# Joining the key and query weights in a routed cross-attention kernel, and moving setup's statistics

## The chip, the core and the metric

The kernel runs on one core of a Trainium2 chip. The time is device microseconds (us) of that core. The engines are PE (TensorE, matrix multiplies; its weight loads are shown as PEld), DVE (VectorE), ACT (ScalarE), POOL (GpSimd) and SP (SyncE, which here only issues transfers). Each engine works through its own list of instructions in order and waits on semaphores for the others. SP, ACT and POOL issue transfers; the queue of SP is q1 in the profile, that of ACT is q10, that of POOL is q0.

## What is computed

There are 8 batches of 512 tokens with 256 features, and 64 context rows per batch. A layer norm of x is followed by attention over the context rows, a router over three experts, the experts, and a gate. All is in 32-bit floats. Cut to what matters here:

```python
nx = layer_norm(x, ln_gamma, ln_beta)
q = nx @ Wq
k = context @ Wk
v = context @ Wv
weights = softmax(einsum('bth,bph->btp', q, k) * H ** (-0.5))
evidence = einsum('btp,bph->bth', weights, v)
combined = concatenate([nx, evidence, cond])
router_probs = softmax(combined @ router_W + router_b)
h = silu(einsum('btc,ecr->bter', combined, e_w1) + e_b1)
expert_out = einsum('bter,erh->bteh', h, e_w2) + e_b2
routed = sum(expert_out * router_probs)
g = sigmoid(silu(combined @ gate_w1 + gate_b1) @ gate_w2 + gate_b2)
out = x + g * (routed @ out_w + out_b)
```

## The kernel before

The batches are taken in pairs (j = 0 to 3). Before the pairs there is a setup, which makes what all pairs use and does the first pair's layer norm, transposes, scores and softmax. Then each pair runs `gate_layer`, `expert_layer` for three experts, and `outputs`; the next pair's layer norm, scores and softmax are placed between these by hand. The order of all engines' instructions is the order in which the program writes them (`manual_schedule`); no planner moves them.

Queries are never made. The scores nx Wq (context Wk)^T are computed as nx times a small matrix per batch, mr, with mr = Wq Wk^T context^T. It has 64 columns for each batch (512 in all), and three further columns of router weights stand beside them. The kernel before makes it in two steps:

- `context_transposes` (L270) turns the context with PE into ctxT, in two halves; DVE copies the first half out of PSUM, ACT the second.
- `project_keys` (L303) multiplies ctxT by Wk, again by halves, into two PSUM banks: eight matmuls of 128x256. ACT copies them to kT (L315).
- `wq_transposes` (L285) transposes Wq with four PE transposes; ACT copies them to wqT (L292).
- `project(wqT, kT, keep_m, "m")` (L1087) makes mr with four matmuls of 128x512; DVE copies each half (L318).

`project` (L294) is also used for v = Wv context (L1078). One 32-bit matmul appears in the trace as two records.

Setup's other work on these lines: `statistics(b, t0, t1)` (L451) runs mean and variance of token blocks t0 to t1 of batch b on DVE, `deviation` (L461) takes the square root on ACT, `normalize` (L464) normalizes x in place on DVE, and `transpose_x` (L486) turns it with PE and scales it on the way out of PSUM, half on DVE (L477) and half on ACT (L481). `small_transposes` (L257) turns the bias rows and cond; `router_anchor` (L324) makes one router row per batch, which POOL writes to memory and reads back spread over the partitions (L332, L333). `scores` (L523) multiplies x by mr. `value_weights` (L622) multiplies v by the second part of the first-layer weights; its router columns go through memory and back on POOL's queue (vrd and vr, L337 and L339) and are read by `router_logits` (L570). `load_table` (L117) runs a one-element activation so that its table is in place early.

PSUM banks in setup are taken in turn by `either` (L244: banks 1, 2, 0, 3) and `misc` (L103: banks 4, 6, 7). The weights and the transposed context live in tiles that later hold the hidden layer and second-layer weights: wk_sb, wq_sb, wqT, wv_sb in one (`scr_w`), kT and the router row in another (`scr_k`). The loads for later weights into the same tiles, `load_anchor(1)` and `load_second(0)`, wait until these are read.

The first transfers are written so: SP issues the context (two halves), x of batch 0, Wq, x of batch 1, then the first-layer weights; ACT issues Wk and Wv; POOL issues the small rows. PE runs seven dummy matmuls first (`wake`, L250).

Of the kernel before, what the change touches and what calls it, by code (L numbers as in the profile page):

```python
# [9 lines left out]
AF = mybir.ActivationFunctionType  # L10
# [6 lines left out]
def kernel(  # L17
# [50 lines left out]
    nc = tc.nc  # L68
    P = 128
    B, T, H = x.shape  # L70
    CT = context.shape[1]
    E, C3, RH = e_w1.shape
    KH = H // P
    NT = T // P
# [22 lines left out]
    def bank(i, name):  # L97
        return psum.tile([P, 512], F32, tag=f"b{i}", name=name)
# [4 lines left out]
    def misc(name):  # L103
        spare.append(spare.pop(0))
        return bank(spare[-1], name)
# [6 lines left out]
    ident = const.tile([P, P], F32, tag="ident", name="ident")  # L112
# [4 lines left out]
    def load_table(func):  # L117
        nc.scalar.activation(warm_t, warm_t, func)
# [5 lines left out]
    def load_x(b):  # L124
        x_sb[b] = xpool.tile([P, NT, H], F32, tag="x", name=f"x_{b}")
        nc.sync.dma_start(x_sb[b], x[b].rearrange("(t p) d -> p t d", p=P))
# [5 lines left out]
    def rows_of(w):  # L132
        return w.rearrange("(k p) n -> p k n", p=P)


    NX = B * CT // P
    HK = KH * RH

    def scratch(i, g, name):
        return h_tile(i, g, name).rearrange("p r t -> p (r t)")  # L140

    def by_k(flat, n):
        return flat.rearrange("p (k n) -> p k n", n=n)

    scr = scratch(1, 2, "scr_ctx")
    ctx_sb, ctxT = by_k(scr[:, :HK], H), by_k(scr[:, HK:], B * CT)
    scr = scratch(1, 1, "scr_w")
    wk_sb, wq_sb, wqT, wv_sb = (by_k(scr[:, i * KH * H : (i + 1) * KH * H], H) for i in range(4))
    scr = scratch(0, 2, "scr_k")
    kT = by_k(scr[:, :HK], B * CT)  # L150
    rrow = scr[:E, HK : HK + B]
    scr = scratch(0, 0, "scr_wa0")
    wa = {0: by_k(scr[:, :HK], RH), E: by_k(scr[:, HK : HK + KH * H], H)}
    scr = scratch(1, 0, "scr_small")
# [80 lines left out]
    vT = const.tile([P, KH, B * CT], F32, tag="vT", name="vT")  # L235
# [8 lines left out]
    def either(name):  # L244
        turn[0] += 1
        return bank((1, 2, 0, 3)[turn[0] % 4], name)
# [10 lines left out]
    def small_transposes():  # L257
        pt = either("pt_rows")
        nc.tensor.transpose(pt[:, :NR], rows, ident[:NR, :NR])
        nc.vector.tensor_copy(cols, pt[:, :NR])  # L260
        pt = either("pt_cond")
        for k in range(KH):
            nc.tensor.transpose(
                pt[:, k * B : (k + 1) * B], cond_sb[:, k * P : (k + 1) * P], ident[:B, :B]
            )
        nc.vector.tensor_copy(
            condT[:, :, :B], pt[:, : KH * B].rearrange("p (k b) -> p k b", b=B)
        )

    def context_transposes():  # L270
        for d in range(2):
            if d:
                wake(1)
            pt = either(f"pt_ctx_{d}").rearrange("p (k c) -> p k c", k=KH)
            for k in range(KH):
                for t in range(NX // 2):
                    nc.tensor.transpose(
                        pt[:, k, t * P : (t + 1) * P],
                        ctx_sb[:, d * (NX // 2) + t, k * P : (k + 1) * P],
                        ident,  # L280
                    )
            half = slice(d * NX // 2 * P, (d + 1) * NX // 2 * P)
            (nc.scalar.copy if d else nc.vector.tensor_copy)(ctxT[:, :, half], pt)

    def wq_transposes():  # L285
        pt = either("pt_wq")
        for k in range(KH):
            for i in range(KH):
                nc.tensor.transpose(
                    pt[:, k * H + i * P : k * H + (i + 1) * P], wq_sb[:, i, k * P : (k + 1) * P], ident  # L290
                )
        nc.scalar.copy(wqT.rearrange("p k n -> p (k n)"), pt)  # L292

    def project(w_sb, src, evacuate, name):  # L294
        for m in range(KH):
            ps = either(f"ps_{name}_{m}")
            for k in range(KH):
                nc.tensor.matmul(  # L298
                    ps, w_sb[:, k, m * P : (m + 1) * P], src[:, k, :], start=(k == 0), stop=(k == KH - 1)
                )  # L300
            evacuate(m, ps)

    def project_keys():  # L303

        ps = [either(f"ps_k_{m}") for m in range(KH)]
        for d in range(2):
            half = slice(d * NX // 2 * P, (d + 1) * NX // 2 * P)
            for m in range(KH):
                for k in range(KH):
                    nc.tensor.matmul(  # L310
                        ps[m][:, half], wk_sb[:, k, m * P : (m + 1) * P], ctxT[:, k, half],
                        start=(k == 0), stop=(k == KH - 1),
                    )
        for m in range(KH):
            nc.scalar.copy(kT[:, m, :], ps[m])  # L315

    def keep_m(m, ps):
        nc.vector.tensor_copy(mr[:, m, :, :CT], ps.rearrange("p (b c) -> p b c", c=CT))  # L318
# [5 lines left out]
    def router_anchor():  # L324
        ps = misc("ps_rb")
        for k in range(KH):
            nc.tensor.matmul(
                ps[:E, :B], rw[:, 2 * KH + k, :], condT[:, k, :B], start=(k == 0), stop=(k == KH - 1)
            )
        nc.vector.tensor_scalar(rrow, ps[:E, :B], rb_c, None, ALU.add)  # L330
        rbd = dram.tile([E, B], F32, tag="rbd", name="rbd")
        nc.gpsimd.dma_start(rbd, rrow)  # L332
        nc.gpsimd.dma_start(rbias, rbd.partition_broadcast(P))  # L333
# [117 lines left out]
    def statistics(b, t0, t1):  # L451
        j, i = b // 2, b % 2
        if b % 2 == 0 and t0 == 0:
            S["mv", j] = work.tile([P, 2, NT, nc.vector.BN_AGGR_DIM], F32, tag="mv", name=f"mv_{j}")
            S["sd", j] = work.tile([P, 2, NT], F32, tag="sd", name=f"sd_{j}")
        for t in range(t0, t1):
            st = work.tile([P, nc.vector.BN_STATS_DIM], F32, tag="st", name=f"st_{b}_{t}")
            nc.vector.bn_stats(st, x_sb[b][:, t, :])
            nc.vector.bn_aggr(S["mv", j][:, i, t, :], st)

    def deviation(j, i):  # L461
        nc.scalar.activation(S["sd", j][:, i, :], S["mv", j][:, i, :, 1], AF.Sqrt, bias=eps_t)

    def normalize(b):  # L464
        mv, sd = (S[n, b // 2][:, b % 2] for n in ("mv", "sd"))
        rstd = work.tile([P, NT], F32, tag="rstd", name=f"rstd_{b}")
        nc.vector.reciprocal(rstd, sd)
        xn = x_sb[b]
        for t in range(NT):
            nc.vector.tensor_scalar(  # L470
                xn[:, t, :], x_sb[b][:, t, :], mv[:, t, 0:1], rstd[:, t : t + 1], ALU.subtract, ALU.mult
            )
        S["xn", b] = xn

    def scale_x(b, k, src, vector):
        if vector:
            nc.vector.tensor_scalar(  # L477
                S["nxT", b][:, k, :], src, gamma_c[:, k : k + 1], beta_c[:, k : k + 1], ALU.mult, ALU.add
            )
        else:  # L480
            nc.scalar.activation(  # L481
                S["nxT", b][:, k, :], src, AF.Identity, bias=beta_c[:, k : k + 1],
                scale=gamma_c[:, k : k + 1],
            )

    def transpose_x(b):  # L486
        xn = S.pop(("xn", b))
        S["nxT", b] = npool.tile([P, KH, T], F32, tag="nxT", name=f"nxT_{b}")
        for k in range(KH):
            pt = misc(f"pt_x_{b}_{k}")  # L490
            for t in range(NT):
                nc.tensor.transpose(pt[:, t * P : (t + 1) * P], xn[:, t, k * P : (k + 1) * P], ident)
            scale_x(b, k, pt, k % 2 == 0)
# [562 lines left out]
    with tc.manual_schedule(engines=None):  # L1056
        ctx_rows = context.flatten_outer_dims().rearrange("(t p) d -> p t d", p=P)
        for d in range(2):
            half = slice(d * NX // 2, (d + 1) * NX // 2)
            nc.sync.dma_start(ctx_sb[:, half, :], ctx_rows[:, half, :])  # L1060
        nc.scalar.dma_start(wk_sb, rows_of(Wk))
        nc.scalar.dma_start(wv_sb, rows_of(Wv))
        load_x(0)
        nc.sync.dma_start(wq_sb, rows_of(Wq))
        load_x(1)
        for g in (E, 0):
            load_first(g)
# [3 lines left out]

        wake(7)
        context_transposes()
        project_keys()
        statistics(0, 0, NT)
        deviation(0, 0)
        normalize(0)
        project(wv_sb, ctxT, lambda m, ps: nc.scalar.copy(vT[:, m, :], ps), "v")  # L1078
        small_transposes()
        wq_transposes()  # L1080
        transpose_x(0)
        router_anchor()
        statistics(1, 0, NT)
        deviation(0, 1)
        normalize(1)
        load_table(AF.Exp)
        project(wqT, kT, keep_m, "m")  # L1087
        combine_weights(E)
        value_weights(0, E)
        spread_router_rows(0)  # L1090
# [131 lines left out]
```

## Time and profile before

| what | value |
|---|---|
| median of 3 runs | 476.01 us (475.64 to 476.08) |
| profiled execution, its own time | 476.25 us |
| span of that execution | 474.5 us |
| ACT busy | 46% of the span |
| POOL busy | 16% of the span |
| transfers | 35.27 MB, mean 74 GB/s over the span |
| transfers in the first 20 us | 6.41 MB, mean 320 GB/s |

The span is the stretch from the first to the last instruction of the profile; the execution's own time is longer by what lies around it. Busy time on PE counts pipelined matmuls whose ends are modelled. In setup (the first 25 us) the groups below have these mean durations for one instruction or record; PE records of successive matmuls overlap, so PE is better read by the distance of their starts.

| line, engine, what | shape | count to 30 us | mean ns |
|---|---|---|---|
| L310 PE matmul, keys | 128x256 | 16 | 394 |
| L298 PE matmul, v | 128x512 | 8 | 592 |
| L298 PE matmul, m | 128x512 | 8 | 605 |
| L289 PE transpose, wq | 128x128 | 4 | 286 |
| L458 DVE statistics | 128x256 | 8 | 400 |
| L459 DVE aggregate | 128x6 | 8 | 182 |
| L470 DVE normalize | 128x256 | 8 | 410 |
| L477 DVE scale | 128x512 | 2 | 806 |
| L318 DVE copy to mr | 128x512 | 2 | 687 |
| L462 ACT square root | 128x4 | 2 | 297 |
| ACT table load | | 4 | 1283 |

### The profile page before, as it was taken

To read this page: it belongs to the slowest core of one execution; us is meant where nothing else is said; L and a number is where in the kernel's file an instruction comes from. 1 tells how busy PE (TensorE), PEld (TensorE's weight loads), DVE (VectorE), ACT (ScalarE), POOL (GpSimd) and SP (SyncE) were. 2 spreads that over 40 slices of the span, in tenths; PEclk is the share of its full clock that TensorE was granted. 3 is DMA by queue.
4 is the path that set the end of the run, shared out by engine and by line. 5 is a ranking of instruction groups with operands and counts; after the bars stand their busy time and mean duration, and the time that the engine had idled before them with its cause. 6 is when DMAs were issued, how large, how long until landed. Compare 5 with 4: busy or idle time off the path is not lost.

```text
span 474.5 us, 4652 instructions
## 1 busy us (share of the span) xinstructions
PE 469.6 (99%) x1451; PEld 225.1 (47%) x1451; DVE 353.4 (74%) x649; ACT 218.4 (46%) x391; POOL 78.2 (16%) x96
## 2 busy tenths in 40 slices
PE   9999999999999999999999999999999999999997
PEld 7654646435454444445454444445454444444454
DVE  2755766989989555889989565898989624697982
ACT  3555656557321546748320456758221365458000
POOL 5227032300062200000062200000042300000020
PEclk9999999999999999999999999999999999999999
DMA  8988330048311840342111750252011560000013
GB/s 285 369 126 159 59 134 1 0 103 104 33 22 22 168 145 0 78 101 44 17 24 22 155 155 2 62 115 46 18 22 22 83 185 0 1 0 1 0 22 67
DMA packets 118120, 35.27 MB, mean 74 GB/s; under 512 B 104732, under 2 KB 115088, under 8 KB 117584
## 3 DMA queue, kind: packets, MB, share of 16 engines
q1 hardware_dynamic: 114736, 27.02, 28.4%
q0 software_dynamic: 1472, 7.18, 4.7%
q10 hardware_dynamic: 1888, 0.79, 0.6%
q8 instruction: 11, 0.18, 0.2%
q14 instruction: 13, 0.11, 0.1%
HBM read 27.57 MB, written 7.40 MB: 74 GB/s over the span
## 4 chain that ended last, share of the span: by engine, by line
PE 94%; DVE 4%; issue 1%; ACT 0%; ACTq 0%
PE ps_u L656 42%; PE ps_z L656 18%; PE ps_y L656 15%; PE ps_vw L631 5%; PE ps_gu L656 3%; PE ps_s L531 3%; PE ps_w2o L416 2%; PE ps_gz L656 1%; DVE h L930 1%; PE ps_wake L255 1%; PE ps_k L310 1%; DVE h L739 1%; PE ps_gy L656 1%; PE ps_v L298 1%; PE ps_ar L354 0%
## 5 line engine op out<-in xcount | busy, mean ns | idle before, releaser
L739 DVE TENSOR_TENSOR h<-h,pb 128x512 f32<-128x512 f32 x96 | 61.9, 693 | 10.5 <-ACT h L689 10.5
L656 PE MATMUL ps_u<-h,w2o 128*128 128x512 f32 x144 | 63.9, 593 | 0.0
L656 PE MATMUL ps_u<-nxT,w 128*128 128x512 f32 x112 | 55.6, 607 | 0.0
L689 ACT ACTIVATE h<-h,abias 128x512 f32<-128x512 f32 x72 | 49.2, 718 | 8.7 <-DVE h L695 8.2
L656 PE MATMUL ps_z<-wT,vw 64*128 64x512 f32 x104 | 49.5, 605 | 0.0
L962 POOL TENSOR_TENSOR yb<-yb,xb 128x512 f32<-128x512 f32 x14 | 19.1, 1365 | 149.5 <-DVE yb L961 145.2
L656 PE MATMUL ps_z<-h,w2s 128*128 128x512 f32 x96 | 42.8, 595 | 0.2 <-DVE r L945 0.2
L698 ACT COPY h<-ps_u 128x512 f32<-128x512 f32 x48 | 28.0, 583 | 32.2 <-PE ps_u L656 31.9
L656 PEld LDWEIGHTS ps_u<-h,w2o 128*128 128x128 f32 x144 | 27.1, 190 | 31.3 <-issue 29.7
L695 DVE TENSOR_TENSOR h<-h,ps_y 128x512 f32<-128x512 f32 x24 | 16.4, 683 | 28.5 <-PE ps_y L656 28.5
L930 DVE TENSOR_TENSOR h<-h,h 128x1024 f32<-128x1024 f32 x24 | 34.3, 1483 | 0.0
L656 PEld LDWEIGHTS ps_u<-nxT,w 128*128 128x128 f32 x112 | 19.9, 189 | 29.7 <-issue 22.8
L689 ACT ACTIVATE h<-ps_u,abias 128x512 f32<-128x512 f32 x24 | 16.5, 687 | 30.4 <-PE ps_z L656 30.4
L656 PE MATMUL ps_y<-nxT,w 128*128 128x512 f32 x56 | 28.6, 592 | 0.0
L656 PE MATMUL ps_z<-T,ws 128*128 128x512 f32 x56 | 28.6, 592 | 0.0
L656 PEld LDWEIGHTS ps_z<-h,w2s 128*128 128x128 f32 x96 | 17.9, 190 | 22.1 <-issue 21.1
L656 PE MATMUL ps_u<-wT,vw 64*128 64x512 f32 x56 | 27.8, 611 | 0.0
L656 PE MATMUL ps_y<-wT,vw 64*128 64x512 f32 x56 | 27.0, 596 | 0.0
L631 PE MATMUL ps_vw<-w,vT 128*128 128x512 f32 (+1 forms) x64 | 26.9, 541 | 0.0
L656 PE MATMUL ps_u<-T,ws 128*128 128x512 f32 x56 | 26.7, 594 | 0.0
L656 PE MATMUL ps_u<-T,w 128*128 128x512 f32 x56 | 26.6, 592 | 0.0
L656 PE MATMUL ps_z<-nxT,ws 128*128 128x512 f32 x56 | 26.6, 592 | 0.0
(206 smaller groups left out, 771.8 us busy)
## 6 DMA issues: line engine op xcount, KB each, us to landing
pb<-pd POOLq DMA_DIRECT2D x4, 1536.0 KB, 7.1
x<-in_x_dram SPq DMA_DIRECT2D x8, 512.0 KB, 5.9
xb<-in_x_dram SPq DMA_DIRECT2D x64, 64.0 KB, 2.5
out_dram<-yb SPq DMA_DIRECT2D x56, 64.0 KB, 2.0
w<-in_L_xcond_e_w_dram SPq DMA_DIRECT2D x6, 512.0 KB, 9.3
xd<-x SPq DMA_DIRECT2D x6, 512.0 KB, 3.0
xg<-xd SPq DMA_DIRECT2D x48, 64.0 KB, 2.4
scr_wa<-in_L_xcond_e_w_dram SPq DMA_DIRECT2D x3, 512.0 KB, 4.7
```

The lines of the kernel that those rows point to most:

```text
L255: nc.tensor.matmul(ps_wake[0][:, :P], zeros, zeros, start=True, stop=True)
L298: nc.tensor.matmul(ps, w_sb[:, k, m * P : (m + 1) * P], src[:, k, :], start=(k == 0), stop=(k == KH - 1))
L416: nc.tensor.matmul(ps[:, d * H : (d + 1) * H], w2T[:, k, (i + d) * P : (i + d + 1) * P], ow_sb[:, k, :], start=(k == 0), stop=(k == KH - 1),)
L531: nc.tensor.matmul(ps[:, t, :], nxT[:, k, t * P : (t + 1) * P], mr[:, k, b, :], start=(k == 0), stop=(k == KH - 1),)
L631: nc.tensor.matmul(ps, vT[:, k, j * 2 * CT : (j + 1) * 2 * CT], w1[:, KH + k, n0:n1], start=(k == 0), stop=(k == KH - 1),)
L656: nc.tensor.matmul(ps, lhsT, rhs, start=start, stop=True, skip_group_check=not start)
L689: nc.scalar.activation(h, h if src is None else src, AF.Silu, bias=abias[:, c, 2 * j + i : 2 * j + i + 1])
L695: nc.vector.tensor_tensor(h, h, part, ALU.add)
L698: nc.scalar.copy(chunk(n, i, d), part)
L739: nc.vector.tensor_tensor(h, h, S["pb", j][:, i, 2 * q // RC, :], ALU.mult)
L930: nc.vector.tensor_tensor(d, p, m, ALU.subtract)
L962: nc.gpsimd.tensor_tensor(yb, yb, S["xb", 2 * j + row][:, i, :], ALU.add)
```

## The change

Wk and Wq are both transposed, and multiplied into one matrix, wkqT; mr is then ctxT times that matrix. The keys are no longer made. `transpose_weights` takes the place of `wq_transposes` and is called for both weights directly after the context's transposes; `join_keys` takes the place of `project_keys` and has four matmuls of 128x256 and one copy on ACT; it stands between the two halves of v. `project` gets a list of the halves to run.

Wq is loaded on ACT's queue between Wk and Wv, not on SP's between the two batches of x. The table of the square root is loaded by a one-element activation directly after ACT's transfers are issued. The statistics of batch 1 run in two halves around `small_transposes`, and the square root of batch 1 comes before `router_anchor` in the program; before, both came after it. The tile `scr_k` now holds wkT and wkqT in place of kT.

```diff
-    kT = by_k(scr[:, :HK], B * CT)
+    wkT, wkqT = (by_k(scr[:, i * KH * H : (i + 1) * KH * H], H) for i in range(2))
     rrow = scr[:E, HK : HK + B]
...
-    def wq_transposes():
-        pt = either("pt_wq")
+    def transpose_weights(dst, w_sb, name):
+        pt = either(f"pt_{name}")
         for k in range(KH):
             for i in range(KH):
                 nc.tensor.transpose(
-                    pt[:, k * H + i * P : k * H + (i + 1) * P], wq_sb[:, i, k * P : (k + 1) * P], ident
+                    pt[:, k * H + i * P : k * H + (i + 1) * P], w_sb[:, i, k * P : (k + 1) * P], ident
                 )
-        nc.scalar.copy(wqT.rearrange("p k n -> p (k n)"), pt)
-
-    def project(w_sb, src, evacuate, name):
-        for m in range(KH):
+        nc.scalar.copy(dst.rearrange("p k n -> p (k n)"), pt)
+
+    def project(w_sb, src, evacuate, name, ms=range(KH)):
+        for m in ms:
             ps = either(f"ps_{name}_{m}")
...
-    def project_keys():
-
-        ps = [either(f"ps_k_{m}") for m in range(KH)]
-        for d in range(2):
-            half = slice(d * NX // 2 * P, (d + 1) * NX // 2 * P)
-            for m in range(KH):
-                for k in range(KH):
-                    nc.tensor.matmul(
-                        ps[m][:, half], wk_sb[:, k, m * P : (m + 1) * P], ctxT[:, k, half],
-                        start=(k == 0), stop=(k == KH - 1),
-                    )
+    def keep_v(m, ps):
+        nc.scalar.copy(vT[:, m, :], ps)
+
+    def join_keys():
+
+        ps = either("ps_kq").rearrange("p (m n) -> p m n", n=H)
         for m in range(KH):
-            nc.scalar.copy(kT[:, m, :], ps[m])
+            for k in range(KH):
+                nc.tensor.matmul(
+                    ps[:, m, :], wkT[:, k, m * P : (m + 1) * P], wqT[:, k, :],
+                    start=(k == 0), stop=(k == KH - 1),
+                )
+        nc.scalar.copy(wkqT, ps)
...
-        nc.scalar.dma_start(wk_sb, rows_of(Wk))
-        nc.scalar.dma_start(wv_sb, rows_of(Wv))
+        for w_sb, w in ((wk_sb, Wk), (wq_sb, Wq), (wv_sb, Wv)):
+            nc.scalar.dma_start(w_sb, rows_of(w))
+        load_table(AF.Sqrt)
         load_x(0)
-        nc.sync.dma_start(wq_sb, rows_of(Wq))
         load_x(1)
...
         context_transposes()
-        project_keys()
+        transpose_weights(wkT, wk_sb, "wk")
+        transpose_weights(wqT, wq_sb, "wq")
         statistics(0, 0, NT)
         deviation(0, 0)
         normalize(0)
-        project(wv_sb, ctxT, lambda m, ps: nc.scalar.copy(vT[:, m, :], ps), "v")
+        project(wv_sb, ctxT, keep_v, "v", (0,))
+        join_keys()
+        project(wv_sb, ctxT, keep_v, "v", (1,))
+        statistics(1, 0, NT // 2)
         small_transposes()
-        wq_transposes()
+        statistics(1, NT // 2, NT)
         transpose_x(0)
+        deviation(0, 1)
         router_anchor()
-        statistics(1, 0, NT)
-        deviation(0, 1)
         normalize(1)
         load_table(AF.Exp)
-        project(wqT, kT, keep_m, "m")
+        project(wkqT, ctxT, keep_m, "m")
         combine_weights(E)
```

## The prediction

> **What bounds the kernel now.** I read the page first: engine totals and the chain that ended last.
>
> ```profile
> span 474.5 us, 4652 instructions
> ...
> PE 469.6 (99%) x1451; PEld 225.1 (47%) x1451; DVE 353.4 (74%) x649; ACT 218.4 (46%) x391; POOL 78.2 (16%) x96
> ...
> PE 94%; DVE 4%; issue 1%; ACT 0%; ACTq 0%
> ```
>
> PE is busy in all but 4.9 us of the span and carries 94% of the chain, so PE time taken out of setup counts, unless another engine or a transfer is already level with PE there. The chain in order of time answers that for setup:
>
> ```profile
> 6.93 3.63 PE ps_k L310 x16
> 10.56 3.43 PE ps_v L298 x8
> 13.99 0.17 PE pt_rows L259
> ...
> 14.27 0.59 PE pt_wq L289 x4
> 14.86 0.45 PE pt_x L492 x4
> ...
> 18.98 1.38 DVE x L470 x4
> 20.36 1.21 DVE mr L318 x2
> 21.57 0.14 issue
> 21.71 3.54 PE ps_s L531 x30
> 25.24 1.77 PE ps_vw L631 x4
> ```
>
> Columns are start, duration, what. PE leads to 15.3 us; then the chain changes to DVE (scale of x 0, statistics of x 1, normalize 1, copies into mr) until the scores start at 21.71; afterwards it is PE again. How much PE lost to DVE is in the timeline:
>
> ```profile
> 7.48 0.43 DVE L458 BATCH_NORM_STATS2 st<-x 128x6 f32<-128x256 f32 x1 [1.18 <-DMA x<-in_x_dram]
> 16.20 0.41 DVE L458 BATCH_NORM_STATS2 st<-x 128x6 f32<-128x256 f32 x1
> 21.12 0.40 PE L531 MATMUL ps_s<-mr,nxT 128*128 128x67 f32 x2
> 21.71 3.54 PE L531 MATMUL ps_s<-mr,nxT 128*128 128x67 f32 x30 [0.19 <-DVE mr L318]
> 33.89 0.56 POOL L339 DMA_DIRECT2D vr<-vrd  x1 [8.35 <-DMA vrd<-vw]
> 45.08 0.55 DVE L576 TENSOR_TENSOR pv<-w,vr 128x384 f32<-128x384 f32 x1
> ```
>
> The first score matmul starts at 21.12, two records of about 0.115 follow, and the third starts at 21.71 where 21.35 was due: a stall of 0.36 us. So PE and DVE are almost level: a PE saving alone would only lengthen this stall, since DVE begins statistics 1 at 16.20, behind the scale. Both halves of the change are needed.
>
> **What the Trainium skill says.** "TensorE: Matmul & The Clock Gate", Part 1, has PE begin at half clock and rise after a busy window of about 3.4 us; its Part 4 says that transposes do not count as busy in the same way. The trace agrees with the first: up to about 7.2 us matmul records of 128x128 and the transposes of the context are 0.21 to 0.23 apart, and the records of ps_k go from 0.43 to 0.22. The second it does not separate: the 3.4 us before that were mostly transposes of the context, and the clock rose all the same. "ScalarE: Activation LUTs", Table sets, says that copy is in every set, so the square root's table can be loaded first and stay through the copies; the trace has two loads of 1.28 (for L283 and L462) before the square root. "DMA: Bandwidth & Descriptors", Queues, rings and completion order, says that each DMA engine serves its queues in turn, packet by packet. The trace agrees: from 3 to 6 us ACT's queue moved 0.22, 0.15 and 0.14 MB, SP's 0.16, 0.23 and 0.20.
>
> **The change part by part.** I use start-to-start distances on PE, which contain the pipeline.
>
> 1. PE, removed. ps_k: 6.72 to 10.39, 3.67 us. The late wq transposes: 14.20 to 14.70, 0.50. Together 4.17.
>
> 2. PE, added. Eight transposes (wk, wq): two groups of 0.50, and about 0.2 more because the first ones run before the clock rises (ps_k paid the same 0.2: 16 records of 0.216 are 3.45). Together 1.2. join_keys: four 128x256 matmuls, 8 records of 0.216, 1.73. Together 2.93. ps_v and ps_m keep their count and shape. Net on PE: 4.17 - 2.93 = 1.24 us less.
>
> 3. The DVE chain. x 0 is now the third transfer on SP's queue as before, but shares the engines with a third weight on ACT's. At 6.0 us SP's queue had 0.33 MB of x 0 left. With Wv's 0.26 MB beside it at 0.38 MB/us in all, Wv finishes near 7.4 and lands near 7.6; x 0 lands near 8.05 instead of 7.45. x 1 has the same bytes before it and lands near 9.7 as now. From there with the durations shown: statistics 0 to 10.3 (2.23), square root 0.3 without a table load, so normalize 0 ends near 12.25 (now 14.42). Half of statistics 1 follows to 13.3, beside PE's v and joined matrix. The small copies end near 13.85, the other half near 14.95, the scale at 15.7, the router row at 15.9, normalize 1 at 17.45 (now 20.36).
>
> 4. PE beside it. Start 6.72, +1.2 transposes = 7.92, v half, join, v half (3.53 + 1.73) = 13.18, small transposes 0.28 = 13.46, x 0 and router 1.14 = 14.60, ps_m 3.54 = 18.14, gate values 0.87 = 19.01, x 1 0.87 = 19.88. Wants: x 1 normalized by 19.01 (have 17.45); second mr copy by 19.9: ps_m ends near 18.3, copy 0.65, so 19.0. Slack 0.9 us: the stall of 0.36 goes, and what is late next is PE itself. The score matmuls then take 3.60 and end at 23.48; now ps_vw follows at 25.08. Gain 1.24 + 0.36 = 1.60.
>
> 5. ACT. The joined copy needs ps_kq (done near 11.4) and stands behind the square root, which waits for statistics 0 until 10.3. Behind that wait are the copies of v's first half, the joined matrix and v's second half; their readers come at 13.3 (the bank for pt_cond), 14.6 (ps_m) and 18.1, so the wait is covered by about 2 us. ACT's three DMA issues (0.5 each) and the table load end near 3.7, its first copy is due at 6.96: nothing. The exp load of 1.28 comes near 15.7 and ACT's next work at about 19: nothing.
>
> 6. SP and POOL. SP has one issue less (0.51) and its waits for older transfers keep their count. The next anchor loads wait for the weights' scratch, free near 13.2 instead of 19.3; the queues were backed up until about 26, so nothing. POOL gets the router row at about 15.9 instead of 16.26, then is paced by the landing of its own small transfers, and does not follow PE. Its last product for this stretch, vr, is issued at 33.89 and lands 7.8 later, at 41.7; DVE reads it at 45.08, which becomes 43.5. Slack falls from 3.4 to 1.8: nothing, with this cover.
>
> Unknown costs. A wait of PE for Wv: at best 0; at worst, if SP's queue takes the larger share, landing near 8.6, 0.7. I take 0 because Wv's and Wk's landings now show about even sharing. The clock's rise: at best the same moment (0), or earlier with another phase of its window, which would give back the 0.2; at worst one or two more windows cold, 1.7 each (half of 3.4), treated as rivals. Join and extra transposes: a group of four transposes on the page's chain is 0.59 rather than 0.50, so 0.2 more at worst. The half statistics between other DVE work: within the slack of 0.9.
>
> Sum against the profiled execution: span 474.5 - 1.6 = 472.9; what lies around the span is 476.25 - 474.5 = 1.75, so 474.65 for that execution. It stands 0.24 above the median of 476.01; from the median the same 1.6 gives 474.4.
>
> **Rivals.** (a) Part of the gain is held up: Wv lands 0.4 to 0.7 after PE asks, or x 0 comes so late that the DVE chain passes its slack of 0.9. For it: three queues' transfers are in flight and PE asks for Wv 2.3 us earlier than now (7.92 against 10.18). Against it: 0.3 us in hand by the shares above, and x 0 would have to come at 9 us. Time: 476.01 - 1.6 + 0.6 = 475.0.
>
> (b) The vr chain on POOL takes the gain back: with DVE 1.6 us earlier and vr late by over 1.8, DVE's in-order queue holds the adds that free PE's banks. For it: POOL does not move with PE, and the landing times of small transfers are long (8.9 for vrd). Against it: those bytes and issue times hardly change. If 1 us of the gain is lost: 475.4.
>
> (c) Slower: the clock. PE's weight transposes take the place of ps_k just where the clock rises. If the matmuls of ps_k were what completed the busy window, and transposes do not count, the clock stays at half for the next window, to about 10.7, which costs 1.7 us: 476.1. That window holds 0.6 us of transposes again, so it may fail too: 3.4 in all, net 1.8 slower, 477.8. It decides from the point where records of ps_v are 0.86 apart instead of 0.43 after 7.9 us. Against it: only about 0.4 us of ps_k lay in the window that raised the clock; the rest was transposes and wake matmuls, which stay.
>
> (d) The change does not do what it says: that copies force another table load between square root and its use. The order of ACT's instructions in the changed program holds one load before the two square roots and one for exp, so no chance is given to it.
>
> **How the numbers follow.** Forecast 0.70, time 474.4; (a) 0.12 at 475.0; (b) 0.06 at 475.4; (c) one window 0.05 at 476.1, two windows 0.07 at 477.8. A measurement here tells 0.2% (0.95 us) from no change: below 475.06 is faster. The forecast with its own spread (0.2 either way for transposes and clock, 0.3 for the runs) is faster nearly always, (a) in two thirds, (b) in a third: 0.78. Same: the rest of (a) and (b) and one cold window, 0.14. Slower: two windows, 0.08. The range goes from 473.7, a clock that rises early with the runs' spread, to 475.4, which takes in (a) and half of (b) and leaves out the cold cases and little else.
>
> **What would show it.** Right: scores start near 19.9 with no stall before their third record, ps_vw behind them near 23.5, mr's second copy ends near 19.0, x 0 statistics begin near 8.0, ps_v near 7.9, only one table load before the first square root. Wrong: an idle PE before ps_v (a), DVE waiting at L576 (b), records of ps_v 0.86 apart (c), or a score start that is early while a later stage of batch pair 0 has a new wait.

## The result, and the profile after

| | median us | runs | range |
|---|---|---|---|
| before | 475.95 | 22 | 475.55 to 476.44 |
| changed | 475.24 | 22 | 475.02 to 475.79 |

The ratio is 0.9987, 95% interval 0.9981 to 0.9993: 0.71 us faster by the medians, less than half of the 1.6 that was forecast. The two profiled executions differ by more, 1.23 us (476.25 and 475.02), because that of the kernel before was slower than its median and that of the changed kernel faster. The profiled execution of the changed kernel took 475.02 us, with a span of 473.2.

The page of the changed kernel, engine totals and the engines' shares of the chain:

```profile
span 473.2 us, 4642 instructions
...
PE 467.6 (99%) x1447; PEld 223.4 (47%) x1447; DVE 353.3 (75%) x649; ACT 217.1 (46%) x391; POOL 78.1 (17%) x96
...
PE 94%; DVE 3%; DMA 1%; issue 0%; ACTq 0%; ACT 0%
```

PE is still the bound, and DVE's share of the chain fell from 4 to 3%. But a transfer, which the chain of before did not name, has 1%. The chain in order of time (start, duration, what) shows which:

```profile
1.79 6.35 DMA scr_w<-in_L_xcond_Wv_dram
8.15 0.14 issue
8.28 1.96 PE ps_v L298 x4
10.24 1.73 PE ps_kq L311 x8
11.96 1.72 PE ps_v L298 x4
...
20.54 3.52 PE ps_s L531 x32
24.06 1.77 PE ps_vw L631 x4
```

From the landing of Wv at 8.15 on, setup is one stretch of PE. Nothing of DVE is in it any more. Some lines of the timeline give PE's wait and its neighbours (in brackets the idle time before the instruction, and what ended it):

```profile
6.34 0.60 PE L289 MATMUL pt_wk<-ident,scr_w 128*128 128x128 f32 x4
6.77 0.60 PE L289 MATMUL pt_wq<-ident,scr_w 128*128 128x128 f32 x4
8.28 1.96 PE L298 MATMUL ps_v<-scr_ctx,scr_w 128*128 128x512 f32 x4 [0.91 <-DMA scr_w<-in_L_xcond_Wv_dram]
8.76 0.43 DVE L458 BATCH_NORM_STATS2 st<-x 128x6 f32<-128x256 f32 x1 [2.45 <-DMA x<-in_x_dram]
18.83 0.69 DVE L318 COPY mr<-ps_m 128x512 f32<-128x512 f32 x1 [0.59 <-PE ps_m L298]
20.38 3.69 PE L531 MATMUL ps_s<-mr,nxT 128*128 128x67 f32 x32
43.82 0.55 DVE L576 TENSOR_TENSOR pv<-w,vr 128x384 f32<-128x384 f32 x1
```

All 32 score records now stand in one group: the stall ahead of the third is gone. DVE waits for PE before its second copy into mr, where PE waited for DVE before. The new wait is the third line: PE has nothing to do from the end of the wq transposes until Wv is there.

### The profile page after: what moved, and what is told of

Same layout as the page of the kernel before. It is cut to its first block, busy times and chain, and to the rows that moved or that the text cites. A ratio compares the mean times of both kernels' runs of the same rounds, so it can differ in the third digit from the quotient of the medians.

```text
span 473.2 us, 4642 instructions
## 1 busy us (share of the span) xinstructions
PE 467.6 (99%) x1447; PEld 223.4 (47%) x1447; DVE 353.3 (75%) x649; ACT 217.1 (46%) x391; POOL 78.1 (17%) x96
## 4 chain that ended last, share of the span: by engine, by line
PE 94%; DVE 3%; DMA 1%; issue 0%; ACTq 0%; ACT 0%
PE ps_u L656 42%; PE ps_z L656 18%; PE ps_y L656 15%; PE ps_vw L631 5%; PE ps_gu L656 3%; PE ps_s L531 3%; PE ps_w2o L416 2%; PE ps_gz L656 1%; DVE h L930 1%; DMA scr_w<-in_L_xcond_Wv_dram 1%; PE ps_v L298 1%; DVE h L739 1%; PE ps_m L298 1%; PE ps_gy L656 1%; DVE r L939 0%; PE ps_ar L354 0%
```

## The experiments

Two theories were tried against each other. W: the wait for Wv takes the missing part. D: the missing part is lost later, behind the late x 0 or in the first pair, and the wait for Wv is covered. In all diffs of this section the lines stand against the changed kernel, unless said otherwise. Ratios are to the kernel before; each of three series of runs had its own runs of that kernel (medians 475.96, 475.89 and 475.65), and gains below are against these.

**Wv ahead of x 0 on SP's queue (v_first, v_first_repeat).**

```diff
-        for w_sb, w in ((wk_sb, Wk), (wq_sb, Wq), (wv_sb, Wv)):
+        for w_sb, w in ((wk_sb, Wk), (wq_sb, Wq)):
             nc.scalar.dma_start(w_sb, rows_of(w))
         load_table(AF.Sqrt)
+        nc.sync.dma_start(wv_sb, rows_of(Wv))
         load_x(0)
```

> The changed kernel, with one transfer moved: Wv goes on SP's queue ahead of x of batch 0, not third on ACT's. Theory W (PE waits for Wv, which lands near 8.15 us, and this wait takes the missing part of the gain): Wv lands near 7.0, ps_v starts at 7.4 to 7.9 straight behind the transposes, and the kernel is 0.35 to 0.9 us faster than the changed one, a ratio to before of 0.997 to 0.998. Rival D (the missing part is lost later, on DVE behind the late x 0 or in the first pair, and the wait for Wv is covered by it): ps_v earlier, but the second score copy or a later wait takes its place, ratio to before unchanged near 0.9987.

Measured: 474.26 us (7 runs), ratio 0.9968, interval 0.9956 to 0.9979. The second series:

> Wv ahead of x of batch 0 on SP's queue once more, for a second interval. Theory W: ratio to before 0.9960 to 0.9975, 474.1 to 474.8 us; ps_v behind the transposes with no wait for a transfer.

Measured: 474.08 us (5 runs), ratio 0.9967, interval 0.9955 to 0.9980. The gains are 1.70 and 1.57 us, and neither interval meets that of the changed kernel; the repeat clears it by 0.0001. The gap to the changed kernel's gain, 0.99 and 0.86, is at the upper end of what W had expected. PE's timeline in v_first:

```profile
6.50 0.60 PE L289 MATMUL pt_wk<-ident,scr_w 128*128 128x128 f32 x4
6.93 0.60 PE L289 MATMUL pt_wq<-ident,scr_w 128*128 128x128 f32 x4
7.37 1.95 PE L298 MATMUL ps_v<-scr_ctx,scr_w 128*128 128x512 f32 x4
9.16 1.89 PE L311 MATMUL ps_kq<-scr_w,scr_k 128*128 128x256 f32 x8
10.88 1.88 PE L298 MATMUL ps_v<-scr_ctx,scr_w 128*128 128x512 f32 x4
...
19.46 3.69 PE L531 MATMUL ps_s<-mr,nxT 128*128 128x67 f32 x32
22.98 1.93 PE L631 MATMUL ps_vw<-w,vT 128*128 128x512 f32 x4
```

ps_v follows the transposes at once, and every later start is 0.9 us earlier than in the changed kernel. The distance from the first ps_v to ps_vw is 15.61 here and 15.62 there (8.28 to 23.90): after ps_v begins, setup is PE's own length. Theory W holds, and this version is faster than both kernels. The move also lets x 0 land earlier (8.41 against 8.73); that this is not what helps is seen below in v_last, where x 0 lands at 7.56 and the kernel is slower than all others.

**Wv later (v_late, v_last).** In v_late the line for Wv stands behind load_x(0), in v_last behind load_x(1).

> The changed kernel, with Wv on SP's queue behind x of batch 0. Theory W: x 0 lands near 7.9, Wv near 8.9, ps_v starts 0.6 to 0.8 us later than in the changed kernel and the whole kernel is later by the same: ratio to before 0.9998 to 1.0005. Rival D: DVE gets x 0 earlier, so the kernel is as fast as the changed one or faster, 0.998 to 0.9987.

Measured: 475.32 us (21 runs), ratio 0.9984, interval 0.9978 to 0.9991: level with the changed kernel, which is what D had expected and outside W's range. In its profile Wv landed at 8.50, not near 8.9, and ps_v began at 8.63, only 0.35 later than in the changed kernel; that execution took 475.72, 0.40 above the median. So the delay was about half of what had been expected, and the run by itself does not speak for W. Therefore the stronger one:

> The changed kernel, with Wv on SP's queue behind both batches of x. In the run with Wv behind x 0 only, Wv landed at 8.5 and not at 8.9, so the test was weak. Here the bytes ahead of it are those ahead of x 1 in the changed kernel, so Wv should land near 9.7 to 10. Theory W: ps_v starts near 9.9, 1.5 us later than in the changed kernel, and all of it is in the time: 476.8, ratio to before 1.0015 to 1.0025. Rival D: less than 0.5 us of it is seen, ratio below 0.9997.

Measured: 478.13 us (4 runs), ratio 1.0041, interval 1.0026 to 1.0056: more than W had asked for. PE's timeline in v_last:

```profile
7.21 0.60 PE L289 MATMUL pt_wq<-ident,scr_w 128*128 128x128 f32 x4
9.99 3.60 PE L298 MATMUL ps_v<-scr_ctx,scr_w 128*128 128x512 f32 x4 [2.19 <-DMA scr_w<-in_L_xcond_Wv_dram]
13.38 1.99 PE L311 MATMUL ps_kq<-scr_w,scr_k 128*128 128x256 f32 x8
```

The start near 9.9 is as expected. But four records of ps_v take 3.39 us from start to start of the next group, where v_first needs 1.79 (7.37 to 9.16). PE's granted clock was 1.00 between 8 and 10 us, 0.54 between 10 and 12, 0.50 from 12 to 13.4 and 0.95 behind that: it had fallen to half after a stretch with only transposes and an idle 2.19 us. This did not happen each time. Three of the four runs had a mean granted clock of 0.995 or 0.996 and took 478.02 to 478.44 us; the fourth had 1.0 and took 476.72, which is W's 476.8. So the long wait for Wv was paid once in all four runs and twice in three, and D, which allowed less than 0.5 us of the delay, is out.

Where the time is lost can also be read from all twelve profiles. In ten of them the execution's time less the start of ps_vw is 451.1 to 451.3 us, with ps_vw starting anywhere from 22.98 (v_first) to 27.30 (v_last). The exceptions are v_late with 451.5 and v_first_no_stats with 452.2, which has a late wait of its own (below). So the time follows the end of setup; later stages add 0.2 us at most in the ten, and about 0.35 in v_late.

**The joined matrix ahead of v (join_first).**

```diff
-        project(wv_sb, ctxT, keep_v, "v", (0,))
         join_keys()
-        project(wv_sb, ctxT, keep_v, "v", (1,))
+        project(wv_sb, ctxT, keep_v, "v")
```

> The changed kernel with the joined matrix made before both halves of v, so that PE asks for Wv 1.7 us later. Theory W: no wait for Wv is left, but the joined matrix needs ACT's second copy, which ended at 8.1 us in the changed kernel; PE starts ps_kq at about 8.2, so nearly nothing is won: 0 to 0.3 us faster than the changed kernel, ratio 0.9980 to 0.9987. If PE's start was held by something else than Wv: the same time with PE idle at another place.

Measured: 475.06 us (21 runs), ratio 0.9985, interval 0.9978 to 0.9991.

```profile
8.81 1.99 PE L311 MATMUL ps_kq<-scr_w,scr_k 128*128 128x256 f32 x8 [0.73 <-ACT scr_w L292]
```

The wait for Wv is gone, and ACT's copy of the transposed Wq stands in its place. (This execution took 475.76, well above the median.) The order by itself wins nothing that the intervals could tell.

**Each half alone.** stats_only is the kernel before with the second half of the change:

```diff
         nc.scalar.dma_start(wv_sb, rows_of(Wv))
+        load_table(AF.Sqrt)
...
+        statistics(1, 0, NT // 2)
         small_transposes()
+        statistics(1, NT // 2, NT)
         wq_transposes()
         transpose_x(0)
+        deviation(0, 1)
         router_anchor()
-        statistics(1, 0, NT)
-        deviation(0, 1)
```

> The kernel before with only the second half of the change: statistics of batch 1 in two halves around the small transposes, the square root ahead of the router row, its table loaded first. By the sum of the prediction the stall of 0.36 us ahead of the third score record goes and PE has no other gain: 0.36 us faster, ratio 0.9992. If the stall only moves to another wait: 1.0000.

Measured: 475.39 us (21 runs), ratio 0.9989, interval 0.9983 to 0.9996. The interval holds the expected 0.9992. The scores in one group, and DVE waiting for PE ahead of its second copy:

```profile
19.38 0.69 DVE L318 COPY mr<-ps_m 128x512 f32<-128x512 f32 x1 [0.61 <-PE ps_m L298]
```
```profile
20.92 3.69 PE L531 MATMUL ps_s<-mr,nxT 128*128 128x67 f32 x32
```

join_only is the changed kernel with the statistics, the square root and its table as they were before (the lines of stats_only the other way round).

> The changed kernel without that second half: statistics of batch 1 behind the router row and no early table load, as before. PE's saving is the same (1.24 us less 0.3 to 0.4 for the wait on Wv, so 0.8 to 0.9), but DVE starts statistics 1 only behind the scale of x 0, so the stall ahead of the scores stays at about 0.4 or grows: 0.4 to 0.8 us faster than before, ratio 0.9983 to 0.9992, with the copies into mr as the last thing the scores wait for. If DVE's order did not matter, it would be level with the changed kernel and the stall gone.

Measured: 475.70 us (13 runs), ratio 0.9995, interval 0.9987 to 1.0003, not told from no change. PE in join_only:

```profile
8.50 1.96 PE L298 MATMUL ps_v<-scr_ctx,scr_w 128*128 128x512 f32 x4 [0.92 <-DMA scr_w<-in_L_xcond_Wv_dram]
...
20.59 0.40 PE L531 MATMUL ps_s<-mr,nxT 128*128 128x67 f32 x2
21.18 3.54 PE L531 MATMUL ps_s<-mr,nxT 128*128 128x67 f32 x30 [0.19 <-DVE mr L318]
```

The wait for Wv is there too (it landed at 8.36), and so is the stall: the third record follows the first by 0.59, exactly as before (21.12 to 21.71). It did not grow although PE came earlier.

**PE's half with Wv in time (v_first_no_stats).** join_only with the loads of v_first.

> Wv ahead of x of batch 0 on SP's queue, but statistics of batch 1 in their old place and no early table load: the sum of PE's saving without DVE's. By the prediction's step on DVE the stall ahead of the third score record is back at 0.4 us or more, since x 0 also lands later than before: ps_v at 7.4, PE ready for scores at 19.5, scores in full only from 19.9 to 20.3. Slower than the kernel with both by 0.4 to 0.7 us, ratio 0.9975 to 0.9985. If PE alone counted, it would be level with the kernel with both, 0.9968.

Measured: 474.50 us (6 runs), ratio 0.9970, interval 0.9958 to 0.9982; 0.24 us above v_first where 0.4 to 0.7 was expected, which the intervals do not tell apart.

```profile
19.68 0.39 PE L531 MATMUL ps_s<-mr,nxT 128*128 128x67 f32 x2
20.26 3.54 PE L531 MATMUL ps_s<-mr,nxT 128*128 128x67 f32 x30 [0.19 <-DVE mr L318]
```

The stall again has its old size: 0.58 between the starts. This profiled execution took 475.85 us, far above its median, because a regrouped block of x for the next pair came late (DVE waited 0.59 us for it at 126.8, and PE 0.47 us for the softmax behind it); only its setup is used here.

**Two more profiles of the unchanged kernels.**

> The kernel before, unchanged, one more profile. Theory: the profiled execution of before that the prediction was made from had a late rise of PE's clock (7.2 us), and its 476.25 is above the median for that. If the clock rises near 6 us here, ps_k should begin near 6.5, take 3.53 instead of 3.67, and the execution should be near 475.7; if it rises late again, near 476.2. Rival: the time does not follow the rise.

Measured: 475.82 us.

```profile
5.88 0.75 PE L277 MATMUL pt_ctx<-ident,scr_ctx 128*128 128x128 f32 x4
6.47 3.69 PE L310 MATMUL ps_k<-scr_ctx,scr_w 128*128 128x256 f32 x16
10.00 1.45 PE L298 MATMUL ps_v<-scr_ctx,scr_w 128*128 128x512 f32 x3
```

Four transposes of the context take 0.59 us from start to start, not 0.91 (5.81 to 6.72 in the execution used for the prediction), and ps_k 3.53, not 3.67: the clock rose earlier, and the execution was 0.43 us shorter. One pair of executions agrees with the theory; it is not a proof that the rise alone makes the spread of the runs.

> The changed kernel, unchanged, one more profile. Theory W: whatever the clock does, ps_v begins about 0.14 us behind the landing of Wv (8.1 to 8.5 us), and ps_vw of batch pair 0 begins 15.6 us behind ps_v. Median executions are at 475.2 to 475.3, so Wv should land near 8.3 and ps_v begin near 8.45.

Measured: 475.02 us. Wv landed at 7.97 and ps_v began at 8.11, 0.14 behind it; ps_vw came 15.61 later, at 23.72. The relation holds; the landing was earlier than the 8.3 expected for a median execution. The time equals that of the first profile although ps_vw came 0.18 earlier: by 37.0 us, in the first pair, the lead is gone (a ps_u record starts at 37.07 here and at 37.03 there). So a small part of a gain can be lost there, as D had it.

## Why the prediction was right or wrong

Sign and range were right: the kernel is faster, and 475.24 lies in 473.7 to 475.4. The forecast of 474.4 was too low by 0.8, and rival (a), given 0.12 at 475.0, is what happened. The prediction gave 0.78 to a time below 475.06, and the median is not below it; that the change is told from none at all is owed to the 22 runs of each kernel.

1. **PE removed and added: right.** With an early clock ps_k takes 3.53 (6.47 to 10.00) and the late transposes 0.49; the early transposes 0.87 (6.50 to 7.37 in v_first) and the joined matrix 1.72 (9.16 to 10.88). The net is 1.43, where 1.24 was forecast from an execution with a late rise; the 0.2 more comes with the early clock of that execution, which the prediction had named as its best case. The stall was a little larger than the 0.36 read: from the first score record to ps_vw it took 3.96 before (21.12 to 25.08) and 3.52 in the changed kernel (20.38 to 23.90), so 0.44. Against this, v in two parts takes 3.60 instead of 3.52 and the transposes of x 1.03 instead of 0.97. Together 1.73; from the start of ps_k in before_look, or of the wk transposes in v_first, to ps_vw the profiles differ by 1.72 (18.20 and 16.48), and by the medians v_first gained 1.70 and 1.57. So the saving exists, once PE is not made to wait.

2. **The step that failed is the landing of Wv**, "Wv finishes near 7.4 and lands near 7.6", and with it the wait of PE, of which the prediction said "I take 0". ACT's queue did move its last packet near 7.4: it ended at 7.51 in the profiled execution, so the shares were right. But Wv landed only at 8.15, 0.64 behind that packet. In the second profile it was 0.51 (7.46 to 7.97), in join_only 0.62 (7.74 to 8.36). The prediction had put 0.2 for this. The trace of the kernel before did not give 0.2: there the queue's last packet ended at 5.68 and Wv landed at 6.14, 0.46 behind. The prediction even used about 0.5 for x 0 in the same step (0.33 and 0.26 MB at 0.38 MB/us from 6.0 on end near 7.55, an estimate from its figures, and its landing was put at 8.05).

   PE also asked earlier than 7.92: the clock had risen during the context's transposes, and the eight transposes took 0.87 instead of 1.2. From the start of the wk transposes to ps_v it took 1.94 us in the profiled execution and 1.45 in the second, against 0.87 without a wait. The wait is therefore 1.07 and 0.58, or 1.09 in join_only (6.54 to 8.50), where 0 was taken and 0.7 was the worst case. From 1.72 this leaves 0.65 to 1.14; the medians say 0.71. Which part of the wait a median execution has was not seen, since only these executions have a profile, and what sets the time between the last packet and the landing was not tried.

3. **"A PE saving alone would only lengthen this stall … Both halves of the change are needed" was wrong.** In join_only and v_first_no_stats PE came earlier and the stall kept its size. The DVE stretch that ends in the copies begins with what PE hands it: in join_only the copy of the small rows waits 1.16 us for PE's transposes and the scale of x 0 another 0.34. So it moves with PE. The kernel before had shown this, ahead of the statistics at 16.20 that the prediction started from:

```profile
15.34 0.81 DVE L477 TENSOR_SCALAR nxT<-pt_x,cols 128x512 f32<-128x512 f32 x1 [0.74 <-PE pt_x L492]
```

   From this scale to the end of the second copy it is 6.23 us before (15.34 to 21.57), 6.23 in join_only and 6.22 in v_first_no_stats. Within the intervals the halves add up. PE's half is worth 1.29 by item 1 without the stall, and v_first_no_stats gained 1.39; the stall is 0.44, and stats_only gained 0.57; PE's half less its wait of 1.09 is 0.20, and join_only gained 0.26, which by itself is not told from nothing.

4. **DVE's order and its slack: right in kind.** x 0 landed at 8.73 and not 8.05, but the second copy into mr still ended 0.86 us before the scores began, and DVE waited for PE ahead of it. With Wv first, slack can run out elsewhere: in v_first_repeat, though not in v_first, PE waits 0.24 us for the copy of cond, which stands behind the first half of statistics 1:

```profile
14.03 0.25 PE L327 MATMUL ps_rb<-condT,rw 128*3 128x8 f32 x4 [0.24 <-DVE condT L266]
```

5. **ACT, SP and POOL at nothing: right.** The square root of batch 0 had no table load ahead of it, and the joined matrix was copied at 12.00, three us before its reader. vr was issued at 34.56 and landed 6.1 later, DVE read it at 43.82 without a wait, so rival (b) did not come.

6. **The clock, rival (c): not in the changed kernel, but real.** Its ps_v records ran at full rate from the first (8.28 to 10.07 for four). v_last shows it behind a longer gap: 1.6 us lost on four records in the profiled execution, and by the mean clock in two of its three other runs. The price of a wait there is not linear.

## What to carry to other kernels

When an edit lets an engine ask earlier for an operand, look up when that operand lands in the trace, and add to its last bytes the time seen between last packet and landing for the same queue (here about 0.5 us); here the wait for this operand was most of what was missing, 1.0 of a possible 1.7 us. Put the load that is needed first ahead of a larger one that is needed later, even on the other queue: moving one line gave back 0.9 us. Before calling two edits dependent, ask where the second engine's stretch starts: if it starts from the first engine's own output, it moves along.

## What the runs showed of the hardware that was not expected

- A load is not there when its last packet is. In the twelve profiles the last load on ACT's queue landed 0.36 to 0.64 us behind the last packet of that queue, in both kernels alike (0.46 and 0.55 before, 0.64 and 0.51 changed), with SP's queue still moving data.
- In v_last PE's clock fell to half (granted clock 1.00, then 0.54 and 0.50) after transposes and an idle stretch of 2.19 us, with no ordinary matmul between the wake-up at 5.5 and 9.99: ps_v records came 0.85 us apart instead of 0.43. One of four runs shows no such fall in its mean clock. In the changed kernel the same stretch ended at 8.28 and the clock stayed up. Which of idle time and transposes counts was not separated.
